# Turning v and the normalized rows on VectorE with block-placing DMAs, in an attention and feed-forward kernel on one Trainium2 core

## Chip, core and metric

The kernel runs on one NeuronCore of a Trainium2 chip. The metric is the device time of one execution in microseconds (us), as the median of several runs. Beside it stands one profiled execution with a trace of every engine: TensorE (PE, its weight loads PEld), VectorE (DVE), ScalarE (ACT), GpSimd (POOL), and SyncE (SP), which only issues DMAs here.

## What is computed

The input x has 4 batches of 1024 rows of 512 values in float32. Two sub-layers follow one another, each normalized before and after:

```
x = x + layernorm(attention(layernorm(x)))
x = x + layernorm(ffn(layernorm(x)))

attention: kqv = x @ Wqkv + bqkv          # 16 heads of 32
           scores = k q^T / sqrt(32), masked to the upper triangle (-10000 below)
           out = softmax(scores)^T v ;  out @ Wo + bo
ffn:       h = silu(x @ Wg^T) * (x @ Wu^T) ;  h @ Wd^T    # 512 -> 2048 -> 512, integer weights minus 128, scaled
```

## The kernel before

The first part is attention, the second the feed-forward net (`ffn`, lines 886 to 1102). Attention handles a batch b in four head blocks hb of four heads (128 columns), and each block in two steps g of 512 queries. Step g = 0 has four tiles c of 128 keys, g = 1 has eight. Each tile is one **period** of the main loop (line 809), 192 in all: 12 per head block, 48 per batch. `at[b, hb, g]` is the first period of a step. In what follows c counts the tiles of a step from 0.

In a period the loop emits, in two halves u = 0 and 1 of two heads each: `weights` (scores of this tile, L370 and L378, into the single `st` buffer, then the exponential L395 on ScalarE and, on tiles at the diagonal, a select L397 on GpSimd); `maxima` (scores for a step 12 periods ahead, L291, reduced by VectorE, L299 and L303); one entry of `later` (divisions and the like); and in one half `values` of the tile before (L417, weights times v). `add_up` adds the exponentials of a step into a sum: tiles 1 to 4 of g = 1 by an accumulating DMA on GpSimd's queue (L445), the narrower ones by GpSimd itself (L447). All queues run in the order in which this Python code emits instructions; SP's too, so a DMA on SP that waits for its data holds up every DMA emitted after it.

Other work is put between these by a small planner. Pieces lie in two kinds of lists, each piece with a cost, a due period and a condition. `lanes` holds projections: q, k ("qk"), v ("v") and the output ("out"), 1.75 units each; `fill` takes them by due period as the budget `spare` allows, up to one in the first half of a period and more at its end. `whole` holds small pieces without cost ("rows", "ln", "turn", "scan"); `fill_whole` takes one per period, in the first half, and if it took one, no projection is filled in there. The functions that matter:

- `ln_load`, `ln_stats`, `ln_norm`, `ln_turn` (L503 to L526): `ln_stage` (L680) works on four row tiles at once, one step each, one stage per period: load 128 rows of x, measure, normalize on VectorE (L88), and turn: four 128 x 128 transposes on TensorE against the identity (L525) into a PSUM bank, copied to `xnT` by ScalarE (L526). The eleven stages of batch 0 run before the loop; those of a later batch may begin 46 periods before its first and are due 24 before.
- `project` (L528): q, k and v of a head block, turned (128 columns on the partitions), 256 rows per piece; `by_columns` (L259) issues its matmuls (L263).
- `turn_v` (L547): v as projected has heads on the partitions, `values` wants rows there. Half of a block's v (512 rows) is turned by four TensorE transposes (L554) into a PSUM bank and copied by ScalarE to `vt` (L555). It is due two periods before the block begins.
- `later_v` (L557): a running sum over v on VectorE.
- `project_out` and `store_out` (L564 to L587): the output projection of one row tile, its layernorm, the residual: x is loaded again as `xo` (L567), GpSimd adds (L586), SP stores to x2 in memory (L587). The store is issued right after the add is emitted.
- `look`, `look_load` (L589 to L600): 48 weight blocks are scanned for their largest value, three periods in four, and the next block is loaded right after.
- `beside` (L250) gives out PSUM banks: the first of a half from `own`, the others from `big`.
- `turned_load` (L92): in the feed-forward part a normalized row tile is stored to memory and read back by four DMAs that put each 32 x 32 block in its place, in runs of 32 values (128 bytes):

```
dst[k * 32 : (k + 1) * 32].rearrange("i c (a r) -> i c a r", r=32),
src.rearrange("(a i) (c k r) -> k i c a r", i=32, k=4, r=32)[k],
```

after which one VectorE instruction (L975) turns every 32 x 32 block within itself. Attention does not use it.

Of the kernel before, what the change touches and what calls it, by code (L numbers as in the profile page):

```python
# [27 lines left out]
def tile_attn_ffn_sandwich(  # L28
# [36 lines left out]
    x3 = dram.tile([B, S, H], F32, tag="x3", name="x3")  # L65
    ident = keep.tile([P, P], F32, tag="ident", name="ident")
# [20 lines left out]
    def normalized(dst, src, mv, i):  # L87
        nc.vector.tensor_scalar(  # L88
            dst, src, mv[:, i, 0:1], mv[:, i, 1:2], ALU.subtract, ALU.mult
        )  # L90

# [18 lines left out]
    with ExitStack() as actx:  # L110
# [116 lines left out]

        actx.enter_context(
# [282 lines left out]
        def ln_norm(b, j):  # L511
            xn = e2.tile([P, H], F32, tag="xn", name=f"xn_{b}_{j}")
            normalized(xn, state.pop(("xr", b, j)), state.pop(("mv", b, j)), 0)
            state["xn", b, j] = xn

        def ln_turn(b, j):
            half, i = divmod(j, NJ // 2)
            if i == 0:
                state["xnT", b, half] = pxn.tile(
                    [P, HC, S // 2], F32, tag="xnT", name=f"xnT_{b}_{half}"  # L520
                )
            xn = state.pop(("xn", b, j))
            pt = beside([P, HC, P], f"xt_{b}_{j}")
            for c in range(HC):
                nc.tensor.transpose(pt[:, c, :], xn[:, ts(c, P)], ident)  # L525
            nc.scalar.copy(state["xnT", b, half][:, :, ts(i, P)], pt)  # L526
# [20 lines left out]
        def turn_v(b, hb, half):  # L547
# [3 lines left out]
            vT = state["v", b, hb]  # L551
            pv = beside([P, 4, P], f"pv_{b}_{hb}_{half}")
            for i in range(4):
                nc.tensor.transpose(pv[:, i, :], vT[:, ts(4 * half + i, P)], ident)  # L554
            nc.scalar.copy(state["vt", b, hb][:, 4 * half : 4 * half + 4, :], pv)  # L555
# [27 lines left out]
        def store_out(b, j):  # L583
# [3 lines left out]
            nc.sync.dma_start(x2[b, j * P : (j + 1) * P, :], xo)  # L587

        def look_load(n):  # L589
            if n < len(blocks):  # L590
                state["look", n] = e2.tile([P, 512], I32, tag="look", name=f"look_{n}")
                nc.sync.dma_start(state["look", n], blocks[n])

        def look(n):
# [5 lines left out]
            look_load(n + 1)  # L600
# [28 lines left out]
        def ffn_stage(i):  # L629
# [10 lines left out]
            if 0 < i <= GT:  # L640
                xn = e2.tile([P, H], F32, tag="xn", name=f"xn2_{i - 1}")
# [37 lines left out]

        def ln_stage(b, j):  # L680

            if j < NJ:
                ln_load(b, j)
# [4 lines left out]
            if 0 <= j - 3 < NJ:  # L688
                ln_turn(b, j - 3)
            count(("ln", b))  # L690

        def normed(b, q):
            return emitted.get(("ln", b), 0) >= NJ // 2 * (q // 2 + 1) + 3
# [8 lines left out]
        for b in range(B):  # L702
            here, after = at[b, 0, 0], at[b, 0, 0] + n_periods // B
            for j in range(NJ + 3):
# [3 lines left out]
                        j - 3 < NJ // 2 or b == 0 or emitted.get(("v", b - 1, HC - 1), 0) >= 2  # L708
                    ),
                    ln_stage, b, j)  # L710
            for hb in range(HC):
# [9 lines left out]
                for q in range(NQ):  # L721
                    put(lanes["v"], FULL, i - 4 - 2 * early,
# [86 lines left out]
        for p in range(-LEAD, n_periods + 1):  # L809
# [7 lines left out]
            state["p"] = p  # L817

# [43 lines left out]
            if p >= 0 and p % 4 != 3:  # L862
# [12 lines left out]
        assert next(looks, None) is None and pre  # L875
        while lanes["out"]:
            piece(lanes["out"])
        assert not any(lanes.values()), lanes
# [267 lines left out]
```

## Time and profile before

| | us |
|---|---|
| median of 3 runs | 1888.07 (1885.6 to 1888.51) |
| profiled execution, its own time | 1883.86 |
| its span | 1882.2 |
| mean granted TensorE clock | 0.993 |
| start of the loop's period 0 (first L370) | 76.4 |
| first feed-forward matmul on the chain of waits | 1171.85 |

The page gives for each engine its busy time, its share of the span and its instructions; then the span in 40 slices of 47 us, each digit a busy share in tenths; then DMA queues, the chain of work that ended last, groups of instructions and DMA issues. In a group's line stand the source line, engine, operation, the names of what is written and read, shapes and count; then busy time, mean nanoseconds of one; then the engine's idle time just before such instructions with what ended it. In a list in order of time the columns are start, length, engine, line, operation; in brackets stands the idle time before and its releaser. In the row of a DMA stand its count, the bytes read and written by one, and the median time from issue to landing.

Two more lines of the page: the accumulations (queue q0) take 18.1% of the time of 16 DMA engines, SP's queue (q1) 14.4%. By engine the chain of work that ended last is PE 84%, DVE 6%, POOL 4%, ACT 2%, DMA 2%.

### The profile page before, as it was taken

Reading aid. Unit: us, or ns where it says so; the run is one execution under the profiler, and the core shown is the slowest. Engines: PE = TensorE matmul, PEld = TensorE weight load, DVE = VectorE, ACT = ScalarE, POOL = GpSimd, SP = SyncE. Lnnn points to the kernel's source line nnn. Section 1 sums busy time; section 2 is a strip of 40 time slices with the busy share of each in tenths; the row PEclk is TensorE's granted clock in tenths of the full one; section 3 lists DMA queues with packets and bytes.
Section 4 is the critical chain, followed back from the end, with each engine's and each line's share of the span. In section 5 each row is a group of like instructions: output and inputs, shape, how many; then the busy total and the mean of one; then the engine's idle time right before and its main releaser. Section 6 shows DMA issues by size and latency. Waiting matters only on the chain.

```text
span 1882.2 us, 40799 instructions
## 1 busy us (share of the span) xinstructions
PE 1810.6 (96%) x17648; PEld 1068.1 (57%) x17649; DVE 1188.9 (63%) x1845; ACT 665.0 (35%) x994; POOL 717.1 (38%) x1000
## 2 busy tenths in 40 slices
PE   7899999999999999999999889999999999999997
PEld 4333444444444444444444335888888888888885
DVE  4688887787676687777677864554544444444433
ACT  2244454444424444424444331222222222222321
POOL 2165655566565566565454664001011010101011
PEclk9999999999999999999999999999999999999999
DMA  3164356435245225334314732532121202121200
GB/s 113 63 138 111 87 123 130 94 94 115 57 101 113 54 61 112 69 93 97 68 36 80 180 96 75 186 100 64 26 75 38 65 20 74 45 45 45 45 23 25
DMA packets 128796, 152.16 MB, mean 81 GB/s; under 512 B 65888, under 2 KB 80224, under 8 KB 128608
## 3 DMA queue, kind: packets, MB, share of 16 engines
q0 software_dynamic: 17280, 62.92, 18.1%
q1 hardware_dynamic: 104176, 82.09, 14.4%
q10 hardware_dynamic: 7152, 4.46, 0.8%
q8 instruction: 140, 2.29, 0.5%
q14 instruction: 48, 0.39, 0.1%
HBM read 62.41 MB, written 24.12 MB: 46 GB/s over the span
## 4 chain that ended last, share of the span: by engine, by line
PE 84%; DVE 6%; POOL 4%; ACT 2%; DMA 2%; issue 1%; SPq 0%; DVEq 0%; POOLq 0%; ACTq 0%
PE pq L263 17%; PE pg L988 12%; PE pu L988 12%; PE acc L1021 12%; PE sc L291 9%; PE po L417 6%; PE st L370 4%; PE py L263 3%; PE st L378 3%; PE pd L428 2%; DMA pT<-pT 2%; ACT pT L395 2%; DVE nm L303 1%; POOL pT L447 1%; POOL xo L586 1%
## 5 line engine op out<-in xcount | busy, mean ns | idle before, releaser
L303 DVE TENSOR_REDUCE nm<-sc 128x2 f32<-128x1024 f32 (+3 forms) x384 | 366.2, 955 | 119.8 <-PE st L378 103.7
L395 ACT ACTIVATE pT<-st 128x1024 f32<-128x1024 f32 (+3 forms) x384 | 310.2, 811 | 346.7 <-PE st L378 268.4
L263 PE MATMUL pq<-xnT,w 128*32 128x256 f32 x6144 | 369.5, 384 | 5.2 <-ACT xnT L526 2.7
L291 PE MATMUL sc<-in,in 32*128 32x512 f32 (+3 forms) x1536 | 345.3, 534 | 6.2 <-DVE y L574 3.5
L378 PE MATMUL st<-in,in 32*128 32x512 f32 (+3 forms) x1536 | 306.0, 487 | 0.0
L263 PEld LDWEIGHTS pq<-xnT,w 128*32 128x32 f32 x6144 | 186.1, 110 | 182.1 <-issue 25.5
L998 DVE SCALAR_TENSOR_TENSOR h<-pu,pre_us,s 128x512 f32<-128x512 f32 x128 | 96.0, 750 | 254.7 <-PE pu L988 254.1
L1021 PE MATMUL acc<-d,h 128*128 128x512 f32 x896 | 221.6, 389 | 0.3 <-DVE h L1008 0.2
L397 POOL TENSOR_SCALAR_AFFINE_SELECT pT<-pT 128x256 f32<-128x256 f32 x256 | 134.5, 536 | 227.8 <-ACT pT L395 227.6
L417 PE MATMUL po<-pT,vt 128*32 128x512 f32 (+3 forms) x1536 | 177.7, 501 | 13.5 <-POOL pT L397 12.4
L1021 PEld LDWEIGHTS acc<-d,h 128*128 128x128 f32 x896 | 168.1, 188 | 35.9 <-DVE h L1008 1.0
L447 POOL TENSOR_TENSOR pT<-pT,pT 128x768 f32<-128x768 f32 (+1 forms) x120 | 187.0, 1578 | 0.0
L299 DVE TENSOR_TENSOR sc<-sc,bound 128x256 f32<-128x256 f32 x256 | 108.5, 424 | 120.5 <-PE sc L291 77.7
L81 POOL TENSOR_SCALAR rs_y<-mv_y 128x1 f32<-128x1 f32 x32 | 8.8, 274 | 434.3 <-DVE mv_y L79 434.3
L996 ACT ACTIVATE s<-pg,pre_gs 128x512 f32<-128x512 f32 x128 | 88.1, 688 | 237.8 <-PE pg L988 237.8
L1007 ACT CAST h<-h 128x512 fp32r<-128x512 f32 x128 | 79.4, 620 | 245.9 <-DVE h L998 245.9
L445 POOL DMA_DIRECT2D pT<-pT x120 | 105.9, 920 | 101.7 <-DMA pT<-pT 49.7
L1008 DVE TENSOR_TENSOR h<-h,h 128x512 fp32r<-128x512 f32 x128 | 88.6, 692 | 87.9 <-ACT h L1007 87.9
L370 PE MATMUL st<-mT,ones_bf 3*128 3x512 bf16 (+3 forms) x768 | 125.3, 331 | 15.1 <-ACT pT L395 14.7
L378 PEld LDWEIGHTS st<-in,in 32*128 32x128 f32 x1536 | 134.1, 190 | 0.2
L263 PE MATMUL py<-wo_sb,o 128*32 128x256 f32 x2048 | 122.5, 387 | 8.9 <-DVE pre_lo L639 4.5
L370 PEld LDWEIGHTS <-ones_bf 3*128 3x128 bf16 x768 | 38.2, 91 | 160.1 <-issue 155.4
(132 smaller groups left out, 2606.2 us busy)
## 6 DMA issues: line engine op xcount, KB each, us to landing
pT<-pT POOLq DMA_DIRECT2D x120, 512.0 KB, 5.5
xr<-in_x SPq DMA_DIRECT2D x32, 256.0 KB, 2.8
xo<-in_x SPq DMA_DIRECT2D x32, 256.0 KB, 2.8
x<-xo SPq DMA_DIRECT2D x32, 256.0 KB, 2.0
out<-y SPq DMA_DIRECT2D x32, 256.0 KB, 2.0
x<-xn SPq DMA_DIRECT2D x28, 256.0 KB, 2.0
xr<-x SPq DMA_DIRECT2D x112, 64.0 KB, 2.5
look<-in_gate_wt SPq DMA_DIRECT2D x16, 256.0 KB, 2.9
```

Of the source, the lines that this page charges most:

```text
L263: nc.tensor.matmul(out[k * D : (k + 1) * D, :], lhsT=lhsT[:, k * D : (k + 1) * D], rhs=rhs, start=(c == 0), stop=(c == len(pairs) - 1),)
L291: nc.tensor.matmul(sc[:, h % 2, :n], lhsT=qT[h * D : (h + 1) * D, ts(j, P)], rhs=kT[h * D : (h + 1) * D, 512 * k : 512 * k + n], start=Tru ...
L299: nc.vector.tensor_tensor(sc[:, :, n - P : n], sc[:, :, n - P : n], bound.unsqueeze(1).to_broadcast((P, 2, P)), ALU.min,)
L303: nc.vector.tensor_reduce(nm[:, k, jj, 2 * u : 2 * u + 2], sc[:, :, :n], AX.X, ALU.max, negate=True)
L370: nc.tensor.matmul(st[h // 2][:, h % 2, :n], lhsT=ones_bf[h * D : h * D + 3, :], rhs=mT[h * D : h * D + 3, 512 - n :], start=True, stop=False,
L378: nc.tensor.matmul(st[h // 2][:, h % 2, :n], lhsT=kT[h * D : (h + 1) * D, ts(c, P)], rhs=qT[h * D : (h + 1) * D, q0 : q0 + n], start=False ...
L395: nc.scalar.activation(pT[:, :, :n], st[u][:, :, :n], AF.Exp)
L397: nc.gpsimd.affine_select(out=pT[:, :, :P], in_=pT[:, :, :P], compare_op=ALU.is_ge, fill=0.0, base=0, pattern=[[0, 2], [1, P]], channel_mu ...
L417: nc.tensor.matmul(state["po"][h * D : (h + 1) * D, 512 - n :], lhsT=v[:, c, h * D : (h + 1) * D], rhs=pT[:, h, :n], start=(c == 0), stop= ...
L447: nc.gpsimd.tensor_tensor(total[:, :, 512 - n :], total[:, :, 512 - n :], pT[:, :, :n], ALU.add)
L988: nc.tensor.matmul(dst, lhsT=w[i * P // IB][:, c, ts(i % (IB // P), P)], rhs=part[:, c, :], start=(c == 0 and k == 0), stop=(c == HC - 1 a ...
L1021: nc.tensor.matmul(acc[t0][t], lhsT=part[:, ts(t, P)], rhs=dw[i * P // IB][:, i % (IB // P), :], start=(i == 0 and k == 0), stop=(i == IC ...
```

## The change

1. **v is turned on VectorE.** `turn_v` makes one VectorE transpose (32 x 32 blocks, each within itself) of half a block's v into `vt`, stores that to a new memory tensor `v_turned`, and reads it back into the same place with four DMAs that move each block to where it belongs. The store is begun one period later, the reads two. v's projections are due one period earlier.
2. **Rows of batches 1 to 3 are turned likewise**, in the other order: the normalized tile is stored to a new tensor x1 (`ln_keep`), read back by `turned_load` (`ln_back`), and turned by VectorE straight into `xnT`. Two stages are added: 13 for these batches. Batch 0 stays as it was. Normalized tiles and those read back share three buffers.
3. **Begun later.** `begin(n, f)` notes f for the start of n periods on; `begin_due` runs it there. The store to x2 is begun one period after its add, or just before the next xo load if that is earlier; the load of the next scanned block one period after the scan, into one buffer in place of two. One period in three scans a block, where it was three in four.
4. **fill_whole** reports whether its piece took a PSUM bank, not whether there was one; so a turn without a bank no longer keeps a projection out of the first half of its period.

```diff
+    x1 = dram.tile([B, S, H], F32, tag="x1", name="x1")
...
+        v_turned = dram.tile([B, HC, 2, P, 512], F32, tag="v_turned", name="v_turned")
...
-        state = {}
+        state = {"p": -LEAD}
+        begun = []
+        def begin(ahead, f):
+            begun.append((state["p"] + ahead, f))
+        def begin_due():
+            for t, f in [w for w in begun if w[0] <= state["p"]]:
+                begun.remove((t, f))
+                f()
...
         def beside(shape, name, dtype=F32):
+            state["banks"] = state.get("banks", 0) + 1
...
         def ln_norm(b, j):
-            xn = e2.tile([P, H], F32, tag="xn", name=f"xn_{b}_{j}")
+            xn = e3.tile([P, H], F32, tag="xn", name=f"xn_{b}_{j}")
...
+        def ln_keep(b, j):
+            nc.sync.dma_start(x1[b, j * P : (j + 1) * P, :], state["xn", b, j])
+        def ln_back(b, j):
+            xr = e3.tile([P, H], F32, tag="xn", name=f"xb_{b}_{j}")
+            xr = xr.rearrange("p (c n) -> p c n", c=HC)
+            turned_load(xr, x1[b, j * P : (j + 1) * P, :])
+            state["xb", b, j] = xr
...
             xn = state.pop(("xn", b, j))
+            if b:
+                nc.vector.transpose(
+                    state["xnT", b, half][:, :, ts(i, P)], state.pop(("xb", b, j))
+                )
+                return
...
         def turn_v(b, hb, half):
-            vT = state["v", b, hb]
-            pv = beside([P, 4, P], f"pv_{b}_{hb}_{half}")
-            for i in range(4):
-                nc.tensor.transpose(pv[:, i, :], vT[:, ts(4 * half + i, P)], ident)
-            nc.scalar.copy(state["vt", b, hb][:, 4 * half : 4 * half + 4, :], pv)
+            vt = state["vt", b, hb][:, 4 * half : 4 * half + 4, :]
+            nc.vector.transpose(
+                vt, state["v", b, hb][:, ts(half, 512)].rearrange("p (c n) -> p c n", n=P)
+            )
+            kept = v_turned[b, hb, half]
+            def back():
+                for k in range(4):
+                    nc.sync.dma_start(
+                        vt[k * D : (k + 1) * D].rearrange("i c (h d) -> i c h d", d=D),
+                        kept.rearrange("(h i) (c k d) -> k i c h d", i=D, k=4, d=D)[k],
+                    )
+            begin(1, lambda: nc.sync.dma_start(kept.rearrange("p (c n) -> p c n", n=P), vt))
+            begin(2, back)
...
         def project_out(b, j, half):
             if half == 0:
+                state.pop("keep_rows", lambda: None)()
...
         def store_out(b, j):
-            nc.sync.dma_start(x2[b, j * P : (j + 1) * P, :], xo)
+            def keep_rows():
+                if state.pop(("kept", b, j), None):
+                    nc.sync.dma_start(x2[b, j * P : (j + 1) * P, :], xo)
+            state["kept", b, j] = True
+            state["keep_rows"] = keep_rows
+            if state["p"] < n_periods - 2:
+                begin(1, keep_rows)
+            else:
+                keep_rows()
...
-                state["look", n] = e2.tile([P, 512], I32, tag="look", name=f"look_{n}")
+                state["look", n] = e1.tile([P, 512], I32, tag="look", name=f"look_{n}")
...
-            look_load(n + 1)
+            begin(1, lambda: look_load(n + 1))
...
+        def turn_at(b):
+            return 5 if b else 3
         def ln_stage(b, j):
+            if b and 0 <= j - 3 < NJ:
+                ln_keep(b, j - 3)
...
-            if 0 <= j - 3 < NJ:
-                ln_turn(b, j - 3)
+            if 0 <= j - turn_at(b) < NJ:
+                ln_turn(b, j - turn_at(b))
+            if b and 0 <= j - 4 < NJ:
+                ln_back(b, j - 4)
...
-                    put(lanes["v"], FULL, i - 4 - 2 * early,
+                    put(lanes["v"], FULL, i - 5 - 2 * early,
...
         def fill_whole(p):
+            banks = state.get("banks", 0)
             if ahead:
                 piece(whole[ahead[0][1]])
-            return bool(ahead)
+            return state.get("banks", 0) > banks
...
             state["p"] = p
+            begin_due()
...
-            if p >= 0 and p % 4 != 3:
+            if p >= 0 and p % 3 == 0:
```

The conditions of the "ln" pieces and of `normed` use `turn_at(b)` in place of 3.

More of the change, by code (lines that the diff above doesn't have):

```diff
@@ L90, in normalized, with turned_load @@
         )
+    def turned_load(dst, src):
+        for k in range(4):
+            nc.sync.dma_start(
+                dst[k * 32 : (k + 1) * 32].rearrange("i c (a r) -> i c a r", r=32),
+                src.rearrange("(a i) (c k r) -> k i c a r", i=32, k=4, r=32)[k],
+            )
     def turned_load(dst, src):
@@ L550, in turn_v @@
                 state["vt", b, hb] = p2.tile([P, NJ, P], F32, tag="vt", name=f"vt_{b}_{hb}")
-            vT = state["v", b, hb]
-            pv = beside([P, 4, P], f"pv_{b}_{hb}_{half}")
-            for i in range(4):
-                nc.tensor.transpose(pv[:, i, :], vT[:, ts(4 * half + i, P)], ident)
-            nc.scalar.copy(state["vt", b, hb][:, 4 * half : 4 * half + 4, :], pv)
+            vt = state["vt", b, hb][:, 4 * half : 4 * half + 4, :]
[4 more added lines that the diff above has]
+            def back():
+                for k in range(4):
+                    nc.sync.dma_start(
+                        vt[k * D : (k + 1) * D].rearrange("i c (h d) -> i c h d", d=D),
+                        kept.rearrange("(h i) (c k d) -> k i c h d", i=D, k=4, d=D)[k],
+                    )
+            begin(1, lambda: nc.sync.dma_start(kept.rearrange("p (c n) -> p c n", n=P), vt))
+            begin(2, back)
         def later_v(b, hb):
@@ L640, in ffn_stage @@
             if 0 < i <= GT:
-                xn = e2.tile([P, H], F32, tag="xn", name=f"xn2_{i - 1}")
+                xn = e3.tile([P, H], F32, tag="xn", name=f"xn2_{i - 1}")
                 normalized(xn, pre["rows"][:, i - 1, :], state.pop(("mv2", i - 1)), 0)
@@ L687, in ln_stage @@
                 ln_norm(b, j - 2)
-            if 0 <= j - 3 < NJ:
-                ln_turn(b, j - 3)
+            if 0 <= j - turn_at(b) < NJ:
+                ln_turn(b, j - turn_at(b))
+            if b and 0 <= j - 4 < NJ:
+                ln_back(b, j - 4)
             count(("ln", b))
         def normed(b, q):
-            return emitted.get(("ln", b), 0) >= NJ // 2 * (q // 2 + 1) + 3
+            return emitted.get(("ln", b), 0) >= NJ // 2 * (q // 2 + 1) + turn_at(b)
         def turn_piece(b, hb, half):
@@ L703, in tile_attn_ffn_sandwich @@
             here, after = at[b, 0, 0], at[b, 0, 0] + n_periods // B
-            for j in range(NJ + 3):
+            for j in range(NJ + turn_at(b)):
                 put(whole["ln"], 0, here - 24,
                     lambda p, b=b, j=j, t=here - 46: p >= t and (
-                        j - 3 < NJ // 2 or b == 0 or emitted.get(("v", b - 1, HC - 1), 0) >= 2
+                        j - turn_at(b) < NJ // 2 or b == 0 or emitted.get(("v", b - 1, HC - 1), 0) >= 2
                     ),
@@ L875, in tile_attn_ffn_sandwich @@
         assert next(looks, None) is None and pre
+        state["p"] = n_periods + 9
+        begin_due()
         while lanes["out"]:
             piece(lanes["out"])
+        assert not begun
         assert not any(lanes.values()), lanes
```

## The prediction, made before the changed kernel ran

> **What bounds the kernel now.** I read the page first: the busy shares and the slices, then busy time by stage, the groups by line, the order of instructions around single transposes, and the DMA rows.
>
> ```profile
> PE 1810.6 (96%) x17648; PEld 1068.1 (57%) x17649; DVE 1188.9 (63%) x1845; ACT 665.0 (35%) x994; POOL 717.1 (38%) x1000
> ...
> PE   7899999999999999999999889999999999999997
> ```
>
> TensorE is busy 96% of the span and nine tenths or more in nearly every slice, and the granted clock is 0.99. By stage (columns: window, its length, busy us of PE, PEld, DVE, ACT, POOL, clock, DMA share, GB/s):
>
> ```profile
> 94.00:517.00 423.00, 410.14 (x5247) 177.13 (x5249) 337.15 (x488) 194.92 (x286) 245.89 (x327) 1.00 0.48 105
> 517.00:564.00 47.00, 42.91 (x619) 20.49 (x611) 35.09 (x62) 12.55 (x20) 31.18 (x42) 1.00 0.43 103
> ```
>
> In attention PE works 97% of the time and VectorE 80%, so VectorE has 86 of 423 us free. The second row is the end of a batch: PE there waits. The feed-forward half, from 1172 us on, is untouched by the change (its PE is full), so everything must come out of the 1170 us before it.
>
> **What is removed.** From the groups by line, with what replaces it (busy us, mean ns of one):
>
> ```profile
> L525 PE MATMUL xt<-ident,xn 128*128 128x128 f32 x128 | 21.9, 296 | 7.9 <-DVE xn L88 6.6 <-DVE y L574 0.6 <-ACT in L545 0.5
> ...
> L554 PE MATMUL pv<-ident,in 128*128 128x128 f32 x128 | 21.0, 286 | 0.8 <-ACT in L545 0.6 <-ACT in L542 0.2
> ...
> L975 DVE STREAM_TRANSPOSE xt<-xr 128x512 f32<-128x512 f32 x28 | 19.7, 704 | 0.0
> ```
>
> All 32 groups of four v transposes (L554) go, and 24 of the 32 row groups (L525; batch 0 keeps its eight). In order of time a group takes 0.59 us from its first transpose to the next instruction: 56 x 0.59 = 33.0 us of PE. But is all of it on the path? Two places in order of time (start us, length us):
>
> ```profile
> 587.49 1.06 PE L417 MATMUL po<-pT,vt 128*32 128x512 f32 x8
> 587.61 1.02 ACT L395 ACTIVATE pT<-st 128x1024 f32<-128x1024 f32 x1 [0.69 <-PE st L378]
> ...
> 588.49 0.66 PE L554 MATMUL pv<-ident,in 128*128 128x128 f32 x4
> ...
> 589.08 0.39 PE L370 MATMUL st<-mT,ones_bf 3*128 3x512 bf16 x2
> ```
>
> ```profile
> 701.95 1.02 ACT L395 ACTIVATE pT<-st 128x1024 f32<-128x1024 f32 x1 [0.69 <-PE st L378]
> ...
> 702.18 0.65 PE L525 MATMUL xt<-ident,xn 128*128 128x128 f32 x4
> ...
> 703.02 0.39 PE L370 MATMUL st<-mT,ones_bf 3*128 3x512 bf16 x2 [0.18 <-ACT pT L395]
> ```
>
> The next scores (L370) go into the one st buffer, which is free only when the exponential of the last ones (L395) has ended, about 0.05 us later. At 587 the exponential ends at 588.63, so without the transposes L370 could start at 588.68 instead of 589.08: 0.40 of 0.59 us is won. At 702 the exponential ends at 702.97 and L370 follows at once: nothing is won. Whole periods say the same: the fifth-tile period with a v transpose runs 592.12 to 597.93 (5.81 us), the one without 658.41 to 663.88 (5.47): 0.34. Going through the 54 groups after 60 us this way, 6 win nothing, 26 win 0.29 to 0.43 (9.6 us together) and 22, whose exponential is done or whose next instruction is L417, win all 0.59 (12.8 us). That is 22.4 us. Eight of the 54 (3.8 us of it) stand at 509-526 and 787-806, where batches end and the chain of waits leaves PE for a pT DMA, L586 and VectorE; I count them as nothing: **-18.6**. The two groups before 60 us lie in the start, with PE idle around them: 0 (at most -1.2). ScalarE loses 56 copies of 586 ns (L526, L555), 32.8 us at a share of 35%: nothing, since PE hardly waits for them.
>
> **What VectorE gains.** 56 transposes x 0.704 = 39.4 us. Outside the batch ends it has 20% idle, and PE waits for its reductions only a few us in all, so it is hidden: a fifth-tile period has two masks, two reductions and about two reciprocals, 2 x (0.43 + 1.23) + 2 x 0.94 = 5.2 us beside 5.8, which a third reader of that engine fills to 5.9 at worst, for one period, with slack after it. At the ends of batches 0 and 1's outputs (517-547 and 796-820) VectorE is on the chain: 2 x 2 v pieces x 0.704 = **+2.8**. The bounds are 0 and, were every one exposed, 39.
>
> **The DMAs.** Each piece adds one 256 KB store and four 64 KB reads of 128-byte runs, all on SP's queue; 56 such pieces. Nearest rows are those of the feed-forward half, which does just this:
>
> ```profile
> pT<-pT POOLq DMA_DIRECT2D x120, 512.0 KB, 5.5
> ...
> x<-xn SPq DMA_DIRECT2D x28, 256.0 KB, 2.0
> xr<-x SPq DMA_DIRECT2D x112, 64.0 KB, 2.5
> ```
>
> Latency: store 2.0, four issues of 0.63 us (L96), landing 2.5: 7.0 us. Who waits? The values (L417) of the first tile of a head block. Following the planner's due times, v's first half is turned four or more periods (20 us) ahead in all but one block: head block 3 of batch 0 turns at 262 us and is read at 271.8, 10 us later, with no pT DMA in between. It fits; 0, at most +4 for that one block. Rows have one stage each for store and read: VectorE could wait for a read if stages lie in adjacent periods (5.6 us each, two of them between normalizing and turning, against 1.65 to 2 us, since a read reuses a buffer whose store is of the same stage, plus 5.0): 0, at most +1 each for about nine.
>
> Here the Trainium skill speaks against the change. "VectorE: DVE Perf Modes", The three transpose paths, says that VectorE turns only 32x32 blocks, that a plain copy whose access pattern does the transposing is 19 times slower than the hardware's own path "when the innermost dest stride is large", and in its rules sends a 128x128 transpose to TensorE. By an estimate from that rule a 256 KB piece would take 19 x 2.8 us (the row load xr<-in_x) = 53 us, over the 20 to 28 us that v has, some 28 us late in 15 blocks, +420 - 22: 2290 us. By the row it takes 7.0. I take the row: same shapes, same 128-byte runs, innermost step one.
>
> Contention: the reads share engines with the pT accumulations. A 256 KB q1 load lands in 2.2 us when that queue rests and in 4 to 5.7 when it works. One piece is 256 KB plus 2048 runs of 13 ns over 16 engines, 0.8 + 1.6 = 2.4 us of all engines; most v pieces are turned in periods 3 and 4 of a second group, so up to 4.8 us falls where accumulations follow one another at 5.5 us each. POOL waits for them already (49.7 us in 28 waits), and the select L397 and the narrow adds L447 stand behind that. Yet the trace holds a trial: in the first five head blocks three to six look and row loads (2.5 to 5 us of all engines) fall in the same window, and the last accumulation lands on average 30.1 us after the first issue; in seven later blocks without them, 29.9. The looks are also thinned from three periods in four to one in three there. I take **+2** (bounds 0 and +42, see below).
>
> **SP's order.** Stores and reads begun at the start of a period stand ahead of that period's xo loads. At batch ends an xo load would wait for a v store or four issues: it lands 2.5 us before its use (538.11 + 2.8 against 543.43). **+1**, bounds 0 and +6. The x2 store moves no further than to just before the next xo load. looks: 48 x 0.67 us as before, over twice as many periods: 0 (-3 to +3).
>
> **Filling.** A turn that takes no bank no longer keeps a projection out of the first half of its period. In some 25 periods one moves there from the end (from the due times), which covers a wait of 0.18 us as at 660.83, and the values close the period: **-2**.
>
> Sum: -18.6 + 2.8 + 2 + 1 - 2 = -14.8. The profiled execution took 1883.86 us (span 1882.2), so 1869; the median of the three runs is 4.2 us above it, and on it the forecast is 1888.07 - 14.8 = **1873**.
>
> **Rivals.** (1) The accumulations do get late. Place: the last two tiles accumulated of each second group. Price: 4.8 us for two pieces, less the slack that the trace shows on the way to PE (1.2 us from the last landing to the narrow add, 0.7 from the last select to the values): 2.9 x 15 = 43, and 43 - 22 gives +20: 1908. It decides from about 1.5 us per block. For it: POOL's slack is small, PE already loses 4.1 us there at 1082. Against it: the trial above. With half that, 1893 to 1900. (2) Nothing comes of it: every slot is bounded by the exponential or VectorE as at 702: 1888. Against: the 5.47 us period. (3) The full slots are won and fills cover every exponential: -33: 1856.
>
> **Chances.** Forecast .54 (1864 to 1883), rival 3 .13 (1855 to 1863), rival 2 .09 (1885 to 1891), rival 1 .24 (1892 to 1910). 0.2%, 3.8 us, is about what a measurement of this kernel can tell. Faster .66, same .10, slower .24. Range 1860 to 1896.
>
> **What would show it.** L554 gone, L525 x32, 84 VectorE transposes near 704 ns; fifth-tile periods with a turn at 5.5 us; feed-forward starting some 15 us earlier. Contention holds if pT's landing stays under 6 us and POOL's wait for it under 65; if it reaches 7 and PE's idle before L417 grows by over 20 us, rival 1 is right. VectorE waiting for xb or PE for vt would refute the latency step.

## The result, and the profile after

The changed kernel takes 1908.43 us (median, 1902.32 to 1910.28) against 1886.84 for the kernel before in the same comparison: ratio 1.012, 95% interval 1.0099 to 1.014, so 21.6 us slower. The profiled execution took 1902.32 us (span 1900.2), 18.5 more than before. The forecast was 1873, and the time is outside the range.

From the page after: busy time by engine, then the slices of TensorE and its granted clock.

```profile
PE 1794.9 (94%) x17423; PEld 1050.1 (55%) x17425; DVE 1220.0 (64%) x1901; ACT 632.0 (33%) x938; POOL 705.1 (37%) x1000
...
PE   7899889999989999889999989999999999999997
...
PEclk9998899999999999999999999999999999999999
```

TensorE has less to do (17423 matmuls for 17648, 15.7 us less busy) and is done later. Slices under nine tenths now stand at 190 to 285, 520, 760 to 855 and 1090 us (a slice is 47.5 us), and in two slices, from 142 to 237 us, the clock is lower. By stage, the same two windows as before:

```profile
94.00:517.00 423.00, 391.84 (x4923) 163.98 (x4917) 319.14 (x472) 170.77 (x249) 224.13 (x311) 0.96 0.58 124
517.00:564.00 47.00, 41.89 (x553) 18.00 (x549) 39.34 (x67) 12.47 (x15) 31.81 (x42) 0.96 0.73 162
```

In the first, 4923 matmuls fit where 5247 did (108 of the missing are the transposes that are gone), and PE is idle for 31 us where it was for 13. The clock is 0.96 there, before it was 1.00.

Where is it? I laid the 192 periods of both traces side by side (from the first scores matmul of one tile to that of the next). The start before period 0 is 5.1 us shorter. Then 48 periods are shorter by 0.2 to 1.0 us each, 22.9 us together; 40 of them, with 18.9 us, held a turn in the kernel before: these are the freed slots, as forecast. Six periods are shorter by more than 1 us, 13.5 us together; five of them shrink as much (by 12.1 us) in the kernel with the new order alone (`neither`, below), so they aren't freed slots. Fourteen periods are longer by more than 1.2 us, 54.2 us together; the longest are at 201 us (+9.3), 259 (+7.6), 465 (+4.8) and 755 (+8.3). The remaining periods add 5.8 us. In sum the loop is 23.5 us longer; what follows it is all but unchanged. The place at 201, in order of time:

```profile
190.35 0.62 SPq L603 DMA_DIRECT2D v_turned<-vt  x1
...
197.05 2.59 SPq L598 DMA_DIRECT2D vt<-v_turned  x4
...
199.74 0.96 SPq L653 DMA_DIRECT2D look<-in_gate_wt  x1
...
200.74 0.44 SPq L541 DMA_DIRECT2D x<-xn  x1
201.23 0.43 SPq L529 DMA_DIRECT2D xr<-in_x  x1
...
203.95 2.60 SPq L107 DMA_DIRECT2D xb<-x  x4
204.55 0.69 DVE L80 BATCH_NORM_STATS2 st_a<-xr 128x6 f32<-128x512 f32 x1 [4.60 <-DMA xr<-in_x]
205.55 0.44 POOL L83 TENSOR_SCALAR rs_a<-mv_a 128x1 f32<-128x1 f32 x1 [3.04 <-DVE mv_a L81]
...
206.61 0.40 POOL L421 TENSOR_SCALAR_AFFINE_SELECT pT<-pT 128x256 f32<-128x256 f32 x1
...
207.07 0.64 PE L441 MATMUL po<-pT,vt 128*32 128x128 f32 x4 [4.09 <-POOL pT L421]
208.50 0.71 DVE L557 STREAM_TRANSPOSE xnT<-xb 128x512 f32<-128x512 f32 x1 [2.58 <-DMA xb<-x]
...
212.05 3.64 PE L287 MATMUL pq<-xnT,w 128*32 128x256 f32 x32
```

Read it as a chain. SP issues v's store at 190.35 and then stands until 197.05, since the next thing on its queue is the read of what it stores. Behind that read come a weight block (L653), the store of one normalized row tile (L541), the load of another (L529) and the turned read of a third (L107). So the load starts at 201.23, right after the store in front of it and with no wait for a buffer; VectorE comes to its statistics and stands 4.60 us. GpSimd is next: in its order the row's variance (L83) is ahead of the causal select (L421), so the select is late, and TensorE stands 4.09 us for the values. Then a second loss: the 32 projection matmuls at 212.05 take 3.64 us where they take 1.93 at full clock. The granted clock of this stretch is 0.81:

```profile
190.00:216.00 26.00, 20.87 (x232) 8.58 (x232) 17.60 (x32) 6.56 (x12) 12.79 (x19) 0.81 0.65 137
```

The waits of VectorE for rows, and those of TensorE that can hang on them, over the whole execution (sum, times, longest). Before, where nothing was read back as xb:

```profile
PE po L417 <- POOL pT L397: 12.4, 13, 4.1
...
DVE st_a L78 <- DMA xr<-in_x: 4.1, 3, 1.5
...
PE py L263 <- DVE y L574: 2.4, 3, 1.4
```

After:

```profile
DVE xnT L557 <- DMA xb<-x: 14.6, 4, 7.6
...
DVE st_a L80 <- DMA xr<-in_x: 10.6, 5, 4.6
...
PE po L441 <- POOL pT L421: 20.4, 19, 4.1
PE py L287 <- DVE y L624: 20.2, 14, 4.3
```

Part of the loss passed at half clock. Between 60 and 1150 us TensorE ran at half clock for 17 us before and for 61 us after. 44 us more at half speed cost up to 22 us. The four executions on record agree with it: their mean granted clock is 0.981 where that of the kernel before is 0.992, and 0.011 of 1908 us is 21 us.

### The profile page after: what moved, and what is told of

The parts are those of the page before. It is cut to its first block, busy times and chain, and to the rows that moved or that the text cites. A ratio compares the mean times of both kernels' runs of the same rounds, so it can differ in the third digit from the quotient of the medians.

```text
span 1900.2 us, 40788 instructions
## 1 busy us (share of the span) xinstructions
PE 1794.9 (94%) x17423; PEld 1050.1 (55%) x17425; DVE 1220.0 (64%) x1901; ACT 632.0 (33%) x938; POOL 705.1 (37%) x1000
## 4 chain that ended last, share of the span: by engine, by line
PE 76%; DVE 9%; POOL 5%; DMA 4%; ACT 3%; issue 2%; SPq 1%; DVEq 0%; POOLq 0%; ACTq 0%
PE pq L287 15%; PE pg L1062 12%; PE pu L1062 12%; PE acc L1095 12%; PE sc L315 8%; PE po L441 5%; PE st L394 4%; PE py L287 3%; DVE nm L327 3%; PE st L402 2%; PE pd L452 2%; ACT pT L419 2%; POOL pT L471 2%; DMA x<-xn 1%; DVE t L516 1%
## 5 line engine op out<-in xcount | busy, mean ns | idle before, releaser
L315 PE MATMUL sc<-in,in 32*128 32x512 f32 (+3 forms) x1536 | 351.6, 543 | 9.0 <-DVE nm L327 8.7
L402 PE MATMUL st<-in,in 32*128 32x512 f32 (+3 forms) x1536 | 311.3, 494 | 0.0
L421 POOL TENSOR_SCALAR_AFFINE_SELECT pT<-pT 128x256 f32<-128x256 f32 x256 | 121.7, 485 | 213.0 <-ACT pT L419 212.8
L441 PE MATMUL po<-pT,vt 128*32 128x512 f32 (+3 forms) x1536 | 176.4, 503 | 22.6 <-POOL pT L421 20.4
L83 POOL TENSOR_SCALAR rs_y<-mv_y 128x1 f32<-128x1 f32 x32 | 8.8, 275 | 434.6 <-DVE mv_y L81 434.6
L469 POOL DMA_DIRECT2D pT<-pT x120 | 106.5, 914 | 127.9 <-DMA pT<-pT 84.7
L287 PE MATMUL py<-wo_sb,o 128*32 128x256 f32 x2048 | 129.1, 398 | 25.1 <-DVE y L624 20.2
L394 PE MATMUL st<-mT,ones_bf 3*128 3x512 bf16 (+3 forms) x768 | 127.0, 336 | 23.4 <-ACT pT L419 21.9
```

The costliest lines, as they stand in the source:

```text
L287: nc.tensor.matmul(out[k * D : (k + 1) * D, :], lhsT=lhsT[:, k * D : (k + 1) * D], rhs=rhs, start=(c == 0), stop=(c == len(pairs) - 1),)
L315: nc.tensor.matmul(sc[:, h % 2, :n], lhsT=qT[h * D : (h + 1) * D, ts(j, P)], rhs=kT[h * D : (h + 1) * D, 512 * k : 512 * k + n], start=Tru ...
L394: nc.tensor.matmul(st[h // 2][:, h % 2, :n], lhsT=ones_bf[h * D : h * D + 3, :], rhs=mT[h * D : h * D + 3, 512 - n :], start=True, stop=False,
L402: nc.tensor.matmul(st[h // 2][:, h % 2, :n], lhsT=kT[h * D : (h + 1) * D, ts(c, P)], rhs=qT[h * D : (h + 1) * D, q0 : q0 + n], start=False ...
L421: nc.gpsimd.affine_select(out=pT[:, :, :P], in_=pT[:, :, :P], compare_op=ALU.is_ge, fill=0.0, base=0, pattern=[[0, 2], [1, P]], channel_mu ...
L441: nc.tensor.matmul(state["po"][h * D : (h + 1) * D, 512 - n :], lhsT=v[:, c, h * D : (h + 1) * D], rhs=pT[:, h, :n], start=(c == 0), stop= ...
```

## Experiments

Theory A: the rows' chain (load, store, turned read, all on SP's one queue) is late for VectorE, which blocks GpSimd and TensorE. Theory B, the prediction's first rival: small transfers delay the accumulations. Theory C: VectorE's added work in its queue. Theory D: the new order alone. All ratios are against the kernel before in the same comparison (its medians are 1884.1 to 1886.8 us, and its half clock is 17 us), with 95% intervals; half clock is the sum between 60 and 1150 us of one profiled execution. What each run changes is told below. Where two ratios are subtracted, the difference is uncertain by some 3 us.

| run | median us | ratio | half clock us |
|---|---|---|---|
| the change | 1908.4 | 1.012 (1.0099 to 1.014) | 61 |
| v_only | 1876.7 | 0.9961 (0.9948 to 0.9973) | 20 |
| rows_only | 1904.4 | 1.0104 (1.0089 to 1.0119) | 55 |
| neither | 1882.6 | 0.9989 (0.998 to 0.9998) | 27 |
| own_xb | 1896.9 | 1.0063 (1.005 to 1.0077) | 58 |
| xr_act | 1904.7 | 1.011 (1.0093 to 1.0126) | 68 |
| own_look2 | 1890.4 | 1.004 (1.0026 to 1.0053) | 51 |
| own_look2_v4 | 1886.2 | 1.0011 (1.0003 to 1.0019) | 41 |
| all_fix | 1893.8 | 1.0041 (1.0028 to 1.0053) | 51 |
| no_row_dma | 1879.2 | 0.9978 (0.9968 to 0.9987) | 41 |
| dma_no_turn | 1887.8 | 1.0021 (1.0011 to 1.0032) | 34 |
| both_turn | 1944.3 | 1.0314 (1.03 to 1.0327) | 65 |
| both_turn2 | 1886.9 | 1.0003 (0.9995 to 1.0012) | 20 |
| rows_act | 1928.5 | 1.0234 (1.0219 to 1.0249) | 78 |
| v_no_dma | 1871.6 | 0.9932 (0.992 to 0.9945) | 20 |
| v_look2 | 1875.0 | 0.9945 (0.9929 to 0.9961) | 27 |
| v_rs_late | 1879.0 | 0.997 (0.9958 to 0.9981) | 34 |
| v_look2_v4 | 1874.7 | 0.9945 (0.9931 to 0.9958) | 27 |

### Which part of the change

v_only takes the rows' part back, rows_only v's part, neither both. The rows' part:

```diff
-            if b:
+            if False:
                 nc.vector.transpose(
...
-            return 5 if b else 3
+            return 3
...
-            if b and 0 <= j - 3 < NJ:
-                ln_keep(b, j - 3)
...
-            if b and 0 <= j - 4 < NJ:
-                ln_back(b, j - 4)
```

v's part:

```diff
-            nc.vector.transpose(
-                vt, state["v", b, hb][:, ts(half, 512)].rearrange("p (c n) -> p c n", n=P)
-            )
...
-            begin(2, back)
...
+            for i in range(4):
+                nc.tensor.transpose(pv[:, i, :], vT[:, ts(4 * half + i, P)], ident)
+            nc.scalar.copy(state["vt", b, hb][:, 4 * half : 4 * half + 4, :], pv)
...
-                    put(lanes["v"], FULL, i - 5 - 2 * early,
+                    put(lanes["v"], FULL, i - 4 - 2 * early,
```

> Only v is turned by VectorE; the rows of the later batches are turned by TensorE as before (no x1 store, no turned read of rows; turning stage 3 again). Theory A (the rows' chain of store, read and turn on SP's one queue is the loss): the long periods at the rows' stages go, v's shorter slots stay, 1868 to 1880 us, under the kernel before. Theory B (the accumulations into pT are late because of all the small transfers): v has 32 of the 56 turned blocks, so more than half of the loss stays, 1885 to 1897. Theory C (VectorE has too much to do): likewise more than half stays, 1885 to 1897.

> Only the later batches' rows are turned by VectorE; v is turned by TensorE as before, with its old due time. Theory A: the whole loss stays and v's gain is missing, 1900 to 1915 us. Theories B and C: less than half of the loss stays, 1885 to 1897.

> Neither is turned by VectorE; what is left of the change is the order: stores and dependent loads begun one period later, weight looks every third period from one buffer, one whole piece no longer keeping the slot closed, three buffers for normalized rows. Theories A, B and C: as the kernel before, 1880 to 1892 us. If the order itself is the loss (theory D): 1897 or more.

All three fall where theory A put them. v is a gain (-7.4 us), the rows alone lose nearly all (+19.6), the order by itself is worth -2. The two parts don't just add: the rows cost 30 us on top of v (1.012 - 0.9961) and 22 us on top of the order alone (1.0104 - 0.9989), so some 8 us of their cost need v's transfers beside them. Theory D is out, and B and C as causes common to v and rows. The first window of the kernel with v alone shows full clock and fewer idle microseconds of PE than after (17 for 31):

```profile
94.00:517.00 423.00, 405.72 (x5199) 172.97 (x5195) 330.76 (x480) 187.56 (x273) 235.55 (x326) 1.00 0.52 111
```

### Rows: transfers, or VectorE's work

no_row_dma drops `ln_keep` and `ln_back` and turns at stage 3. It leaves out the placing of the blocks:

```diff
-                    state["xnT", b, half][:, :, ts(i, P)], state.pop(("xb", b, j))
+                    state["xnT", b, half][:, :, ts(i, P)], xn.rearrange("p (c n) -> p c n", c=HC)
```

both_turn and both_turn2 go on from there to TensorE's four transposes; both_turn copies the result into `xn`, both_turn2 into a tile of its own, with two buffers for `xn` to make room:

```diff
-                return
...
                 nc.tensor.transpose(pt[:, c, :], xn[:, ts(c, P)], ident)
+            if b:
+                nc.scalar.copy(e1.tile([P, HC, P], F32, tag="idle", name=f"idle_{b}_{j}"), pt)
+                return
```

> The whole change, but the later batches' rows are turned by VectorE straight from the normalized row, two stages earlier (where TensorE turned them), without the store and the turned read: the blocks are not placed, so the rows of batches 1 to 3 are the reference's only within blocks of 32, and the output differs. VectorE's work on rows stays, their 120 transfers go. Theory A: the loss goes and the shorter slots of the rows come on top of v's, 1866 to 1877 us. Theory C (VectorE's added work in its queue): the loss stays, 1892 or more.

> The kernel in which VectorE turns rows without their transfers, with TensorE's turning of the same rows and ScalarE's copy put back beside it (TensorE's result goes into the normalized row, which nobody reads again; what reaches the projections is VectorE's, so rows of batches 1 to 3 are right only within blocks of 32). Against the kernel with v alone it has 24 VectorE transposes of 0.70 us more and nothing less. If VectorE's added work costs (theory C in part): 1880 to 1890 us, and the freed TensorE slots were worth the difference to 1879. If freed TensorE slots at the rows' stages were worth nothing, and TensorE's idling there halves its clock: 1874 to 1879, with less half clock than the 41 us of the kernel without TensorE's turning.

> The kernel in which VectorE turns rows without their transfers (1879.2 us), with TensorE's turning of the same rows put back beside it, ScalarE's copy now going into a tile of its own that nobody reads, so that no engine waits for another's turn. Rows of batches 1 to 3 are right only within blocks of 32. Against the kernel with v alone (1876.7) it has 24 VectorE transposes of 0.70 us more and nothing less. If TensorE's freed slots at the rows were worth their 0.34 to 0.59 us each and VectorE's work costs as much: 1885 to 1890. If the freed slots were worth nothing (TensorE waited there anyway) and VectorE's transposes cost nothing by themselves: 1875 to 1880, with half clock down from 41 us towards the 20 us of v alone.

Without the rows' transfers 1879.2: between the two expectations, near A. So 1.012 - 0.9978 = 1.42%, 27 us, are the transfers and what waits for them. The periods say where: the four longest, 30.0 us too long in the change, are 2.2 us too long here, while the other ten are 24.2 us too long in both kernels. And it isn't the accumulations: they land as late without the rows' transfers as with them (the change, then no_row_dma):

```profile
pT<-pT POOLq DMA_DIRECT2D x120, 512.0 KB, 6.3
```

```profile
pT<-pT POOLq DMA_DIRECT2D x120, 512.0 KB, 6.2
```

But the rows' shorter slots did not come on top of v's gain either. both_turn could not say why: it made ScalarE wait for VectorE's turn, and TensorE for ScalarE.

```profile
ACT xn L564 <- DVE xnT L557: 78.6, 24, 6.6
PE pq L287 <- ACT xn L564: 50.6, 18, 5.9
```

both_turn2 has no such wait, and its 1886.9 falls in the first of the two ranges. Against v alone it only adds 24 VectorE transposes of 0.70 us (16.9 us), with one buffer fewer for normalized rows: +0.42%, 7.9 us, as much as half of them exposed. Against it no_row_dma takes away 24 TensorE turns and their copies (and, with no bank taken, lets projections into those half periods): -0.25%, 4.7 us, where 24 slots of 0.34 to 0.59 us should give 8 to 14. One place shows where some of the rest may have gone. First with TensorE's turning (v alone), then without (no row transfers), the same stretch of the program in order of time:

```profile
159.78 0.41 PE L441 MATMUL po<-pT,vt 128*32 128x128 f32 x4 [1.29 <-POOL pT L421]
160.12 0.66 PE L563 MATMUL xt<-ident,xn 128*128 128x128 f32 x4
160.71 0.39 PE L394 MATMUL st<-mT,ones_bf 3*128 3x512 bf16 x2
160.72 0.70 PE L315 MATMUL sc<-in,in 32*128 32x512 f32 x2
...
160.93 0.59 PE L402 MATMUL st<-in,in 32*128 32x512 f32 x2
```

```profile
159.06 0.64 PE L441 MATMUL po<-pT,vt 128*32 128x128 f32 x4 [1.85 <-POOL pT L421]
159.63 0.61 PE L394 MATMUL st<-mT,ones_bf 3*128 3x512 bf16 x2
159.65 1.23 PE L315 MATMUL sc<-in,in 32*128 32x512 f32 x2
160.03 1.06 PE L402 MATMUL st<-in,in 32*128 32x512 f32 x2
```

TensorE waits for GpSimd's select in both. Without the transposes it waits 0.56 us longer, and from 158.7 us the clock is half for 10.2 us: a scores matmul pair takes 1.06 us for 0.59. Freed time in a stretch that TensorE doesn't bound is idle time, and here half clock followed. In all, the profiled execution has 41 us at half clock here and 20 in both_turn2. But these are single executions: over all executions on record the mean granted clock is 0.9884 (22 executions) against 0.9899 (13), a difference worth up to 3 us. So clock explains at most a part of what is missing; the rest is not shown.

### Which queue holds the transfers

own_xb:

```diff
-            xr = e3.tile([P, H], F32, tag="xr", name=f"xr_{b}_{j}")
+            xr = p4.tile([P, H], F32, tag="xr", name=f"xr_{b}_{j}")
...
-            xn = e3.tile([P, H], F32, tag="xn", name=f"xn_{b}_{j}")
+            xn = state["xr", b, j]
...
-            xr = e3.tile([P, H], F32, tag="xn", name=f"xb_{b}_{j}")
+            xr = e2.tile([P, H], F32, tag="xb", name=f"xb_{b}_{j}")
```

xr_act:

```diff
-            nc.sync.dma_start(xr, x[b, j * P : (j + 1) * P, :])
+            (nc.scalar if b else nc.sync).dma_start(xr, x[b, j * P : (j + 1) * P, :])
```

> The whole change, but a row that is read back has a buffer pair of its own: the row is normalized in place (four buffers), so that the read of one row no longer takes the buffer of the next row, which is being stored in the same stage. Theory A in its narrow form (the read waits for that store, SP stands behind it, VectorE stands for the read): the four waits of VectorE for a read row (14.6 us) and the half clock after them go, 1885 to 1897 us. Theories B and C: nothing of their cause is touched, 1902 to 1910.

> The whole change, with one thing moved: the loads of the later batches' rows (24 transfers) are issued from ScalarE's queue and not from SP's. Theory A as a queue (a row's load stands on SP behind v's store and reads, behind the weight look and behind the turned read of another row, and VectorE stands for it with POOL behind): VectorE's 10.6 us of waits for a loaded row and what follows them, above all the nearly 10 us at 200 to 215 us, go; the waits for a row read back (14.6 us) stay: 1892 to 1900 us. If the transfers themselves are slow (contention with the accumulations): 1902 to 1910, with the waits as before.

own_xb gains 0.57%, 10.7 us. The read of row j takes, in the change, the buffer of row j + 1, whose store is issued in the same stage: SP's turned reads wait less for stores, and the 27 waits that are left are the feed-forward's (the change, then own_xb):

```profile
SPq L107 <- DMA x<-xn: 84.0, 40, 7.3
```

```profile
SPq L107 <- DMA x<-xn: 46.3, 27, 3.0
```

But the expectation that both VectorE's waits and the half clock after them would go was too much: waits for rows read back fell from 14.6 to 6.5 us, those for loaded rows rose from 10.6 to 15.3, and half clock stayed (58 us for 61).

xr_act misses. VectorE hardly waits for loaded rows:

```profile
DVE xnT L557 <- DMA xb<-x: 22.4, 5, 7.2
...
DVE st_a L80 <- DMA xr<-in_x: 3.0, 3, 1.5
```

It waits for rows read back instead, in the same places; near 200 us:

```profile
196.88 2.75 SPq L598 DMA_DIRECT2D vt<-v_turned  x4
...
204.53 2.60 SPq L107 DMA_DIRECT2D xb<-x  x4
...
209.47 0.71 DVE L557 STREAM_TRANSPOSE xnT<-xb 128x512 f32<-128x512 f32 x1 [6.97 <-DMA xb<-x]
```

Load and turned read stand behind the same v read; setting one free leaves VectorE standing for the other. So the mend has to be in what they stand behind.

own_look2 is own_xb with the first of these edits, own_look2_v4 with both:

```diff
-            begin(1, lambda: look_load(n + 1))
+            begin(2, lambda: look_load(n + 1))
...
-            begin(2, back)
+            begin(4 if half else 2, back)
```

> The kernel with rows normalized in place and a buffer pair for rows read back, and the load of the next weight look begun two periods after the look and not one, so that SP no longer stands at it for VectorE's last work of a period before it comes to the rows' transfers. Theory A as a queue: the rows' chains start earlier, VectorE's waits for rows (15.3 and 6.5 us in that kernel) shrink by half or more: 1880 to 1892 us. If the queue is not it: 1894 to 1900, as that kernel.

> The whole change with own buffers for rows read back and looks begun two periods on (1890.4 us), and the turned read of v's second halves begun four periods after the turn and not two: v's values of that half are needed only in the second step, and SP no longer stands for v's store (6.5 us at 193 to 200 us) in front of the rows. If that standing is what is left of the rows' lateness: the 6 us at the period of 24 (11.7 us long) and part of the later ones go, 1880 to 1886. If not: 1888 to 1892.

dma_no_turn turns the rows on TensorE at stage 3, as v_only, but keeps `ln_keep` and `ln_back` (one stage more). rows_act is own_xb with `nc.scalar.dma_start` in `ln_load`, `ln_keep` and the four reads of `ln_back` for batches 1 to 3:

```diff
-            for j in range(NJ + turn_at(b)):
+            for j in range(NJ + (4 if b else 3)):
```

```diff
-            nc.sync.dma_start(x1[b, j * P : (j + 1) * P, :], state["xn", b, j])
+            nc.scalar.dma_start(x1[b, j * P : (j + 1) * P, :], state["xn", b, j])
```

> The reverse: TensorE turns the later batches' rows as before, but each row is still stored and read back turned, into tiles that nobody uses. The 120 transfers and their places on SP's queue stay, VectorE waits for none of the rows read back, but still for the rows loaded. If a wait for a row read back is what matters: near the kernel with v alone, 1875 to 1882. If the queue (loads late behind stores and reads) or contention matters: 1886 to 1897, with waits for a loaded row near 10 us.

> The whole change with rows normalized in place and a buffer pair for rows read back, and all transfers of the later batches' rows (load, store and the four of the turned read) issued from ScalarE's queue; v, looks and output rows stay on SP. Theory A as a queue (what makes a row's chain late is its place behind v's transfers and the looks on SP): VectorE's waits for rows all but go, and what is left is as without the rows' transfers, 1878 to 1889 us, some of it ScalarE's own issuing (24 stages by some 3 us, beside its exponentials). If the chain of store, read and landing is too long by itself: 1893 or more, with waits for rows read back of 6 us and more.

own_look2 gains another 0.23% (4.3 us). SP stood 255.9 us at the looks for VectorE's scan in own_xb and 175.4 here; VectorE's waits fall from 15.3 to 11.5 us for loaded rows and from 6.5 to 2.1 for rows read back, in sum not by the half that I expected. own_look2_v4 gains 0.29% (5.5 us), though its 1886.2 just misses what I wrote. In it the rows near 200 us go ahead of v's second half: the load that started at 201.23 in the change starts at 190.92.

```profile
190.92 1.51 SPq L529 DMA_DIRECT2D xr<-in_x  x1
192.47 5.54 SPq L107 DMA_DIRECT2D xb<-x  x4
...
203.48 2.67 SPq L598 DMA_DIRECT2D vt<-v_turned  x4
```

The period at 201 us, 6.3 us too long in own_look2, is back to its old length, but its two neighbours are now 2.0 and 1.4 us too long. The sum over the four longest periods of the change follows the mends: 30.0 us too long in the change, 22.4 in own_xb, 15.3 in own_look2, 9.3 in own_look2_v4, 2.2 in no_row_dma. Together the three mends take back 20.5 of the 27 us without removing one transfer: so most of it is the order on SP. What is left, 0.33% or 6 us against no_row_dma, holds what these runs don't split: the transfers' bandwidth, and what is still late (the periods at 465 and 755 us remain 3.7 and 6.1 us longer than before).

dma_no_turn says that the transfers cost something even when VectorE waits for no row read back: 1.0021 against 0.9961 for v alone, 11 us. The four periods are only 1.6 us too long in it, so these 11 us lie elsewhere. They aren't the late loads that I expected either: VectorE waits 6.3 us for loaded rows, in v_only 7.8. The accumulations land in 6.5 us against 6.1, and GpSimd waits 82.6 us for them against 69.1, which points to theory B for this part; no run tests it by itself. (The unused reads may overwrite a later row in their buffer: some rows of this kernel's output are wrong. The work is as listed.)

rows_act is a miss that teaches: ScalarE's queue is in order too. Its exponentials stood behind the waits of the rows' transfers, and TensorE behind the exponentials (sum, times, longest; in the change TensorE waited 21.9 us here).

```profile
PE st L394 <- ACT pT L419: 73.3, 56, 7.8
ACT pT L419 <- DMA xb<-x: 47.9, 12, 8.9
```

### v, and versions that are faster

v_no_dma is v_only without v's store and read; it leaves out the placing of v's blocks. v_look2 and v_look2_v4 are v_only with the mends of the last section. v_rs_late and all_fix are v_look2 and own_look2_v4 with GpSimd's two operations of a row's variance emitted a period later.

```diff
-            begin(1, lambda: nc.sync.dma_start(kept.rearrange("p (c n) -> p c n", n=P), vt))
-            begin(2, back)
```

```diff
+            def rstd():
+                rs = p4.tile([P, 1], F32, tag="rs", name=f"rs_a{b}_{j}")
+                nc.gpsimd.tensor_scalar_add(rs, mv[:, :, 1], EPS)
+                nc.gpsimd.tensor_tensor(mv[:, :, 1], rs, minus_half, ALU.pow)
+            begin(1, rstd)
```

> The kernel with v alone on VectorE, without v's store and turned read (160 transfers less): v's blocks are not placed, so the weighted sums of v are the reference's only within blocks of 32 tokens by 32 columns, and the output differs. Theory B for v (the small transfers delay the accumulations): 1866 to 1873 us. Theory A: v has its transfers far enough ahead, 1874 to 1879.

> The kernel with v alone on VectorE and the next weight look's load begun two periods after the look. If SP standing at the look delays rows' loads there too (VectorE waits 7.8 us for loaded rows): 1870 to 1876 us. If not: 1875 to 1879.

> The kernel with v alone and the later look loads (1875.0 us), and the two small operations that POOL does for a row's variance (add, power) emitted at the start of the next period, so that POOL no longer stands in front of its causal selects for VectorE's statistics of a row (32 us in 23 waits, 3.7 at most). If that stand reaches TensorE (13.7 us of waits of the value products for POOL): 1868 to 1873 us. If it is covered: 1873 to 1877.

> The whole change with the four mends: own buffers, looks two periods on, second halves of v read back two periods later, and POOL's variance of a row one period later. With SP's order and POOL's order both out of the way what is left is VectorE's work on the rows: 1872 to 1880 us, under the kernel before. If VectorE standing for rows remains: 1883 or more.

> v alone on VectorE, weight looks loaded two periods on, and the turned read of v's second halves begun four periods after the turn: the two mends of SP's order that helped the whole change, on the part of the change that was a gain. If SP standing for v's store costs there too (v's transfers were worth 5 us when left out): 1869 to 1874 us, the fastest with the reference's whole work. If with the rows' transfers gone nothing is behind that stand: 1873 to 1878.

v's own 160 transfers cost 0.29%, 5.5 us, more than twice the price I gave contention, and the time falls where theory B put it. B's mark is there too (accumulations land in 6.1 us with them, 5.6 without; GpSimd waits 69.1 and 62.5 us), but the run takes away v's places on SP as well and doesn't split the two. Emitting GpSimd's variance a period later missed twice, slower by 0.25% (against v_look2) and 0.30% (against own_look2_v4). In all_fix the wait has turned round: GpSimd stands 17.3 us for statistics where it stood 35.0 in own_look2_v4, but the normalizing on VectorE stands for GpSimd.

```profile
DVE xr L90 <- POOL mv_a L545: 10.9, 6, 3.1
```

In v_rs_late the same wait is only 3.8 us, and why that kernel is slower stays open. v_look2 and v_look2_v4 have the lowest medians with the whole work, 0.9945 both: v on VectorE, rows left on TensorE. v_only's interval overlaps theirs, so that the later looks help here is not shown; 1875.0 lies in both of v_look2's ranges. The later v read, worth 5.5 us with rows behind it, shows no gain without them: SP's stand for v costs through what is queued behind it.

## Why the prediction was wrong

In ratios against the kernel before, the change's +22.6 us (1.012) are -7.4 for v, +7.9 for VectorE's work on the rows, -4.7 for the rows' freed slots and +27 for their transfers with the waits for them.

- **Slots, -18.6 (-22.4 with the batch ends):** right as a sum over periods: 22.9 us in 48 periods, 18.9 of them where a turn had been. What I did not weigh is that a freed slot where TensorE waits for something else is idle time: for the rows 4.7 us (uncertain by some 2) were left of 8 to 14.
- **The start, 0 (at most -1.2):** -5.1 in the profiled execution, -4.9 with v alone, +0.6 with rows alone, +0.4 with neither. It belongs to v, but its size isn't steady: the other kernels with v on VectorE have -1.5 to -4.9.
- **Rows' latency, "0, at most +1 each for about nine":** this step failed. The transfers and their waits cost 27 us (1.42%), and the sign that I had named against it came: VectorE waits 14.6 us for xb. I compared 1.65 to 2 plus 5.0 us with two periods of 5.6 us, as if each transfer started at the start of its stage's period. I had even named the shared buffer, but only as latency of this row. But the queue is in order: the wait for a buffer or for a store is not only this row's, it is that of every transfer behind it. Mended, the order gives back 20.5 us. With the wait misjudged, feed-forward starts 18.4 us later and not some 15 earlier.
- **SP's order, +1:** I looked only at xo loads behind v's transfers, not at rows behind v's transfers and looks. It is the same error seen from the queue.
- **VectorE, +2.8 (bounds 0 and 39):** too small. 24 row turns alone cost 7.9 us (both_turn2 against v_only, intervals of some 3 us). A busy share of 80% was taken for 20% of cover. Why half of it is exposed no run shows; that a row's statistics, normalizing and turn stand in front of one period's reductions is my reading of the order.
- **Contention, +2 (bounds 0 and 42):** too small in the same direction; up to 5.5 us for v. By the signs that I named contention as forecast is refuted (pT lands in 6.3 us, not under 6; GpSimd waits 84.7 us, not under 65), but rival 1's signs didn't come either: the landing didn't reach 7 us, and TensorE's idle time before the values grew from 13.5 to 22.6 us, not by over 20.
- **Rival 1 (1908):** the number is near the measured one, but not by its mechanism. The 27 us lie in four periods with stages of rows and go with the rows' transfers, while the accumulations' landing stays (6.3 and 6.2 us); and v alone, which has more than half of the turned pieces, is a gain.
- **The clock:** no step reckoned with it. All four of the longest periods run into half clock (from 206, 264, 472 and 762 us on). Up to 22 us of the loss passed that way; this is no further term, it lies within those above.
- **The rule of 19 times** was rightly set aside: the turned reads land in 2.8 us (rows) and 3.7 us (v), medians, not in 53. (The estimate had set the rule on a row load, while the rule compares with the hardware's own transposing path.)
- **Filling, -2:** not tried by itself.

## What to carry to other kernels

Before giving an in-order queue new transfers, write out the queue's whole order around them: a transfer starts only after all waits in front of it, so a dependent load (store, then read back) belongs as late as its reader allows, and a shared buffer counts as a wait for everybody behind. Work taken from the busiest engine is worth only what it bounds, place by place, and idle gaps can cost as much again in clock (up to 22 us here). If one wait is removed and the time stays, look for the second one behind the same cause.

## What the runs showed of the hardware

The clock changes in steps of 3.41 us: up to 1150 us every half-clock stretch of every trace here is 3.4, 6.8 or 10.2 us long. I took TensorE's busy share in the 3.41 us ahead of each change. In the change's trace all ten drops to half clock come after a share of 0.54 or less (0.06 to 0.54); of the windows at full clock that were followed by full clock, two had 0.50 and 0.54 and all others 0.57 or more. It came back only after a share of 0.90 or more, and stayed half after shares of up to 0.97. The trace of the kernel before has one drop after 0.71, its other four after 0.52 or less, and one return after 0.84; so these shares give no exact threshold. The Trainium skill ("TensorE: Matmul & The Clock Gate", Part 1) says that half clock follows an idle window of some 3.4 us. The step agrees. The window didn't have to be wholly idle, though: if it had, none of the ten drops would have come. About half idle was enough here, so a stall of some 2 us can cost clock when it falls within one window.
